# Sorting the listed columns of a sparse graph kernel by the half of the block's rows they reach, and multiplying half-width tiles in layer 2

## The chip, the cores and the metric

The kernel runs on one core of a Trainium2 chip. The metric is the time on the device in microseconds. The kernel before took 1107.85 us (median of three runs, 1107.15 to 1109.62). The profile is one further execution under the profiler, which took 1219.48 us; its span is 1217.8 us. A timed run is thus some 110 us shorter than what the profile shows.

## The reference, cut to what matters

The input is a feature matrix x of 2708 rows and 512 columns, and a sparse adjacency matrix adj (2708 x 2708) whose row density falls from the first rows to the last. Four layers follow each other, each of them x = layernorm(x + layer(x, adj)):

```python
# layer 0: normalized adjacency, then a projection
h = (d[:, None] * (adj + eye) * d[None, :]) @ x @ W.T + b
# layer 1: adj plus a head weight where adj > 0, by the degree
(inc @ x) / inc.sum(axis=1)
# layer 2: two gated branches over the same adj
h = x @ W_sa
e = where(adj != 0, exp(-leaky_relu(s_left[:, None] + s_right[None, :], 0.01)), 0)
x_a = (e / (e.sum(axis=1) + 1e-5)) @ h
x_b = adj @ (x @ W_gcnb) + b_gcnb
sigmoid(attn_a * x_a + attn_b * x_b)        # attn_* are gates from adj @ x and x
# layer 3: signs of x times signs of the weight, then adj, then relu
relu(adj @ (max(sign(x), 0) @ sign(weight).T))
```

All of it is fp32. Layer 2 needs, for each row, two weighted sums over its neighbours: one with the weights adj and one with the weights e.

## The kernel before, in words

Rows are cut into 22 blocks of 128 (the last has 20). For each block b other than 0 the kernel finds the columns of adj in which any of the block's 128 rows has an entry, lists them, and from then on works only on these. The list is padded to a fixed number of tiles of 128 columns, ROOM[b], from 9 for block 1 down to 4 and 1; in all there are 107 listed tiles. A few blocks treat block 0's columns (and block 1 its own) as whole tiles as well, which DIRECT names; block 0 itself uses all columns. A block's own diagonal is handled apart where it is the only entry (own_by_itself).

**First stage.** A loop of turns, one block per turn (function turn), reads adj in row blocks and finds the lists. Its instructions keep their written order on each engine (in_order). For a block, mark writes a 0/1 mask of the row block, and 22 products with a column of ones (line 801) count for each column how many of the block's rows have an entry. For a group of up to three blocks (GROUPS), count turns these counts into hits, numbers them with a scan along the free axis (line 820), and builds a table; count_partitions (line 833) adds the partitions in front; steps_of takes differences between partitions (line 849); look_up compares slot numbers with each partition's start (line 865) and multiplies (line 870) so that each slot of the list learns which column it holds. list_nodes writes the indices, and POOL then gathers the listed columns of adj (line 928) into packed[b]. The same turns transpose and project x for layer 0 (lines 943 and 958).

**Layers 0 and 1** gather feature rows by the indices (line 570) and multiply each tile of packed[b] with them.

**Layer 2** (function parts_of_sums and what follows) cuts a block's tiles into parts of up to three tiles. prepare makes, for one part, a buffer ae with two halves for each tile: adj itself and the weights e. The work is done by weights_of (lines 1326 to 1330: score plus bias on ScalarE, leaky relu, mask and sum on VectorE, exp on ScalarE), a copy (line 1474) and a reduction into esum (lines 1476 to 1487). There are three ae buffers. accumulate multiplies: add_products (line 1337) takes a gathered tile of 128 feature rows as the stationary operand, in four column chunks, and moves both halves of ae past it, 2 x 128 columns, into the accumulator acc. Gathered rows come by POOL's indirect DMA (line 1492) into seven buffers. project2 then copies acc to SBUF (pt, line 1520), multiplies with wab (pc, line 1527), W_gcnb and W_sa (pg and ph, line 1534), finish2 gates and normalizes (with a power on POOL, line 621), and sign_product (lines 1578 and 1583) prepares layer 3. Two parts of the next block are prepared ahead of the present block's projections in program order; the engines then run in the order that a scheduler gave their instructions at compile time.

**Layer 3** multiplies by tiles of the same packed[b] (lines 1694 and 1736).

Of the kernel before, what the change touches and what calls it, by code (L numbers as in the profile page):

```python
# [8 lines left out]
F32 = mybir.dt.float32  # L9
# [25 lines left out]
          13: (0,), 14: (0,), 15: (0,), 16: (0,), 17: (0,)}  # L35

# [449 lines left out]
def sparse_layers(ctx, tc, x, adj, adj_t, w0_t, b0, w_sa, a_sa, w_gcnb, b_gcnb, wa, ba, wb, bb, w3_t,  # L486
# [9 lines left out]

    nc = tc.nc
# [44 lines left out]
    ones_b = const.tile([P, 1], BF16, name="s_ones_b")  # L542
    nc.vector.memset(ones_b, 1.0)
# [6 lines left out]
    found = const.tile([P, NB], F32, name="s_found")  # L550
# [95 lines left out]
    l01 = ctx.enter_context(ExitStack())  # L646
    heads = l01.enter_context(tc.tile_pool(name="s_heads", bufs=1, reuse_waits="tile"))
    head_row = heads.tile([P, N], F32, name="s_head_row")

    with tc.tile_pool(name="s_pre", bufs=1) as pre:  # L650
        TM = max(ROOM)
        TS = max(sum(ROOM[b] for b in g) for g in GROUPS)
        GM = max(len(g) for g in GROUPS)
        NT = NB + 3
# [47 lines left out]
        )  # L702
        step = pre.tile([P, P], BF16, name="s_step")
# [3 lines left out]
        )  # L707
        off_dia = pre.tile([P, P], BF16, name="s_off_dia")
# [12 lines left out]
        lane_i = pre.tile([P, GM], I32, name="s_lane_i")  # L721
        nc.gpsimd.iota(lane_i, pattern=[[0, GM]], base=0, channel_multiplier=1)
        lane = pre.tile([P, GM], BF16, name="s_lane")
        nc.vector.tensor_copy(lane, lane_i)
        keep = pre.tile([P, GM, NB], BF16, name="s_keep")
# [38 lines left out]

        search = {}
        group_of = {b: g for g in GROUPS for b in g}

        def mark(b: int):
# [4 lines left out]
            if i == 0:  # L773
                find = ps_s.tile([P, D], F32, tag="find", name=f"find{b}", bufs=2)
                n = len(g)
                search[g] = {
                    "hits": find[:, : n * NB].rearrange("p (g s) -> p g s", g=n),
                    "before": find[:, n * NB : n * (NB + 1)],
                    "diff": find[:, D // 2 : D // 2 + n * NT],
                }  # L780
# [19 lines left out]
            for s in range(NB):  # L800
                nc.tensor.matmul(
                    search[g]["hits"][:, i, s : s + 1], mask[:m, s * P : (s + 1) * P], ones_b[:m],
                    start=True, stop=True,
                )

        def own_diagonal(b: int):

            if own_by_itself(b):
                g, m = group_of[b], rows(b)
                nc.vector.scalar_tensor_tensor(  # L810
                    dia_own[:m, b : b + 1], search[g]["hits"][:m, g.index(b), b : b + 1], 0.0,
                    dia[:m, b : b + 1], op0=ALU.is_equal, op1=ALU.mult,
                )

        def count(g):
            b0_, G = g[0], len(g)
            hit = small.tile([P, GM, NB], BF16, tag="hit", name=f"hit{b0_}")
            nc.vector.tensor_scalar(hit[:, :G], search[g]["hits"], 0.0, None, op0=ALU.is_gt)
            turn = small.tile([P, GM, NB], F32, tag="turn", name=f"turn{b0_}")
            nc.vector.tensor_tensor_scan(  # L820
                turn[:, :G].rearrange("p g s -> p (g s)"),
                keep[:, :G].rearrange("p g s -> p (g s)"),
                hit[:, :G].rearrange("p g s -> p (g s)"), 0.0, op0=ALU.mult, op1=ALU.add,
            )
            nc.vector.tensor_copy(found[:, b0_ : b0_ + G], turn[:, :G, NB - 1])
            table = small.tile([P, GM, NT], BF16, tag="table", name=f"table{b0_}")
            nc.vector.tensor_tensor(table[:, :G, :NB], turn[:, :G], hit[:, :G], op=ALU.mult)
            nc.vector.tensor_copy(table[:, :G, NB + 2], lane[:, :G])
            search[g].update(table=table)

        def count_partitions(g):
            b0_, G = g[0], len(g)
            nc.tensor.matmul(
                search[g]["before"], tri, found[:, b0_ : b0_ + G], start=True, stop=True
            )

        def steps_of(g):
            b0_, G = g[0], len(g)
            table, diff = search[g]["table"], search[g]["diff"]
            base = small.tile([P, 2, GM], F32, tag="base", name=f"base{b0_}")  # L840
            nc.vector.tensor_copy(base[:, 0, :G], search[g]["before"])
            nc.vector.tensor_scalar(
                base[:, 1, :G], base[:, 0, :G], WHOLE128, WHOLE128, op0=ALU.add, op1=ALU.subtract
            )
            nc.vector.tensor_copy(table[:, :G, NB], base[:, 1, :G])
            nc.vector.tensor_tensor(
                table[:, :G, NB + 1], base[:, 0, :G], base[:, 1, :G], op=ALU.subtract
            )
            nc.tensor.matmul(
                diff, step, table[:, :G].rearrange("p g c -> p (g c)"), start=True, stop=True  # L850
            )
            search[g]["base"] = base

        def look_up(g):
            b0_, G = g[0], len(g)
            base, diff = search[g]["base"], search[g]["diff"]
            steps = small.tile([P, GM, NT], BF16, tag="steps", name=f"steps{b0_}")
            nc.scalar.copy(steps[:, :G], diff.rearrange("p (g c) -> p g c", g=G))
            looked = ps_s.tile([P, D], F32, tag="looked", name=f"looked{b0_}", bufs=1)
            T = sum(ROOM[b] for b in g)  # L860
            lv = looked[:, : T * NT].rearrange("p (t c) -> p t c", t=T)
            after = pre.tile([P, TS * P], BF16, tag="after", name=f"after{b0_}", bufs=1)
            at = 0
            for i, b in enumerate(g):
                nc.vector.tensor_scalar(
                    after[:, at * P : (at + ROOM[b]) * P], slot[:, : ROOM[b] * P],
                    base[:, 0, i : i + 1], None, op0=ALU.is_ge,
                )
                for t in range(at, at + ROOM[b]):
                    nc.tensor.matmul(  # L870
                        lv[:, t, :], after[:, t * P : (t + 1) * P], steps[:, i, :],
                        start=True, stop=True,
                    )
                at += ROOM[b]
            search[g]["looked"] = lv
# [257 lines left out]
        room = pre.tile([1, NB], F32, name="s_room")  # L1133
        for b in range(NB):
            nc.vector.memset(room[:, b : b + 1], float(P * ROOM[b]))
        tot = ps_s.tile([P, D], F32, tag="find", name="tot", bufs=2)
        nc.tensor.matmul(tot[0:1, :NB], ones, found, start=True, stop=True)
        n_over = const.tile([1, 1], F32, name="s_n_over")
        nc.vector.tensor_tensor(room, tot[0:1, :NB], room, op=ALU.is_gt)
        nc.vector.tensor_reduce(n_over, room, axis=AX.X, op=ALU.add)  # L1140

    work = ctx.enter_context(tc.tile_pool(name="s_work", bufs=2, side="right", reuse_waits="tile"))
# [189 lines left out]
    def add_products(b: int, src, ae, r: int, is_first: bool, is_last: bool):  # L1332

        m = rows(b)
        acc = state[b]["acc"]
        for k in range(KC):
            nc.tensor.matmul(  # L1337
                acc[:, k, :].rearrange("p (h i) -> p h i", h=2)[:, :, :m],
                src[:r, k * P : (k + 1) * P], ae[:r, :, :m],
                start=(is_first and k % 2 == 0), stop=(is_last and k % 2 == 1),  # L1340
            )
# [17 lines left out]
    with tc.tile_pool(name="s_l1", bufs=8, reuse_waits="tile") as lp:  # L1359
# [4 lines left out]
        def grow2(j: int, n: int):  # L1364
# [15 lines left out]
            add_products(0, f[j], ae, r, n == 0, n == NB - 1)  # L1380
# [36 lines left out]
    with tc.tile_pool(name="s_l2o", bufs=1, reuse_waits="tile") as op, \  # L1417
# [6 lines left out]

        def parts_of_sums(b: int):

            runs = [(i, min(CH, tiles(b) - i)) for i in range(0, tiles(b), CH)]
# [4 lines left out]
        def prepare(b: int, c: int):  # L1432
# [5 lines left out]
            if run is None:  # L1438
# [3 lines left out]
                st["own_ae"] = ae  # L1442
# [14 lines left out]
                nc.scalar.activation(ae[:m, 1, :m], ident[:m, :m], AF.Copy, scale=own[:m, 4:5])  # L1457
                st["ae"][c] = ae
                return
            i0, n = run  # L1460
            nd = len(direct(b))
            for i in range(i0, i0 + n):
# [4 lines left out]
            a = packed[b][:, i0 : i0 + n, :]  # L1467
            ae = lp.tile([P, CH, 2, P], F32, tag="ae", name=f"ae{b}_{i0}", bufs=3)
            av, ev = ae[:, :n, 0, :m], ae[:, :n, 1, :m]
            weights_of(  # L1470
                ev, av, sl[:, :m], a, [st["src"][i][:, D : D + 1] for i in range(i0, i0 + n)],
# [3 lines left out]
            if i0 == 0:  # L1475
# [3 lines left out]
                if own_by_itself(b):  # L1479
                    own_e = st["own_ae"][:m, 1, :m]  # L1480
                    nc.vector.tensor_tensor(esum[:m, :m], esum[:m, :m], own_e, op=ALU.add)
            else:
                part = lp.tile([P, P], F32, tag="part", name=f"part{b}_{i0}")
                nc.vector.tensor_reduce(
                    part[:, :m, None], ev.rearrange("p t i -> p i t"), axis=AX.X, op=ALU.add
                )
                nc.vector.tensor_tensor(esum[:, :m], esum[:, :m], part[:, :m], op=ALU.add)
# [10 lines left out]
        def accumulate(b: int, c: int):  # L1498
# [6 lines left out]
            if run is None:  # L1505
                add_products(b, f[b], ae, m, True, last)
                return
            i0, n = run
            for i in range(n):
                add_products(  # L1510
                    b, st["src"][i0 + i], ae[:, i], P, c == 0 and i == 0, last and i == n - 1
# [312 lines left out]
```

## Time and profile before

| | value |
|---|---|
| timed, median of three | 1107.85 us |
| span of the profiled run | 1217.8 us |
| TensorE busy | 1007.9 us, 83% |
| VectorE busy | 726.2 us, 60% |
| POOL busy | 533.5 us, 44% |
| ScalarE busy | 403.4 us, 33% |
| products of line 1337 on gathered tiles | 856 instructions, 187.9 us |
| chain that ended last | PE 31%, DVE 5%, DMA 5% |

The profile's lines name an engine (PE is TensorE, PEld its weight loads, DVE VectorE, ACT ScalarE, POOL GpSimd), a line of the kernel, what is written from what, the shapes, the count, the busy time with the mean duration of one, and the idle time ahead with what ended it. Busy time of products is counted from their issue to their modelled end, and successive products overlap, so a product's mean duration is not the pace at which they follow each other. The chain is followed back from the last instruction to what released it at each step. The page also cuts the span into 40 slices with one digit of busy share each.

### The profile page before, as it was taken

To read this page: it belongs to the slowest core of one execution; us is meant where nothing else is said; L and a number is where in the kernel's file an instruction comes from. 1 tells how busy PE (TensorE), PEld (TensorE's weight loads), DVE (VectorE), ACT (ScalarE), POOL (GpSimd) and SP (SyncE) were. 2 spreads that over 40 slices of the span, in tenths; PEclk is the share of its full clock that TensorE was granted. 3 is DMA by queue.
4 is the path that set the end of the run, shared out by engine and by line. 5 is a ranking of instruction groups with operands and counts; after the bars stand their busy time and mean duration, and the time that the engine had idled before them with its cause. 6 is when DMAs were issued, how large, how long until landed. Compare 5 with 4: busy or idle time off the path is not lost. (4 is left out here: it accounts for less than half of the span.)

```text
span 1217.8 us, 13502 instructions
## 1 busy us (share of the span) xinstructions
PE 1007.9 (83%) x4009; PEld 608.2 (50%) x4028; DVE 726.2 (60%) x2556; ACT 403.4 (33%) x869; POOL 533.5 (44%) x545
## 2 busy tenths in 40 slices
PE   3865677579789789989799999999999999698852
PEld 2432333123334234445566677676666666476631
DVE  4764556464567676778656655656555554346765
ACT  4542444100000044668533223223232322243420
POOL 0455544676666377675332233222221211066660
PEclk9877778789799899999899999999999999889976
DMA  9875775476677677776332223223121211199982
GB/s 330 297 230 182 222 228 157 113 243 200 199 201 224 188 202 207 216 218 205 87 84 75 66 74 97 65 57 88 51 85 40 79 40 53 57 338 287 256 238 80
DMA packets 84523, 193.53 MB, mean 159 GB/s; under 512 B 13680, under 2 KB 26968, under 8 KB 84440
## 3 DMA queue, kind: packets, MB, share of 16 engines
q0 software_dynamic: 41056, 113.12, 33.8%
q1 hardware_dynamic: 31692, 64.45, 15.5%
q10 hardware_dynamic: 11692, 15.01, 3.8%
q8 instruction: 34, 0.56, 0.2%
q14 instruction: 49, 0.40, 0.1%
HBM read 155.73 MB, written 25.92 MB: 149 GB/s over the span
## 5 line engine op out<-in xcount | busy, mean ns | idle before, releaser
L1492 POOL DMA_INDIRECT xg<-x_rows,i x107 | 106.1, 991 | 216.9 <-DVE mv L619 63.3
L1337 PE MATMUL acc<-ae,xg 128*128 128x256 f32 x856 | 187.9, 378 | 0.4 <-ACT ae L1330 0.3
L1337 PEld LDWEIGHTS acc<-ae,xg 128*128 128x128 f32 x856 | 161.9, 190 | 23.0 <-ACT ae L1330 1.1
L928 POOL DMA_INDIRECT a<-in_adj_t_dram,row_at x107 | 110.2, 1030 | 128.6 <-DVE mask L782 83.6
L570 POOL DMA_INDIRECT xg<-x_rows,i x107 | 113.0, 1056 | 57.3 <-issue 26.2
L570 POOL DMA_INDIRECT xg<-y_rows,i x107 | 105.6, 987 | 53.3 <-issue 24.3
L1398 PE MATMUL l<-xg,inc 128*128 128x512 f32 x214 | 103.0, 617 | 15.6 <-DMA xg<-x_rows,i 12.4
L1254 PE MATMUL l<-xg,a 128*128 128x512 f32 x214 | 109.6, 645 | 7.6 <-issue 4.1
L570 POOL DMA_INDIRECT xg<-xw_rows,i x83 | 82.9, 998 | 46.1 <-issue 20.4
L958 PE MATMUL y<-s_w,xt 128*128 128x512 f32 (+1 forms) x176 | 96.1, 692 | 2.2 <-issue 2.0
L1534 PE MATMUL pg<-s_wg,pt 128*128 128x512 f32 (+1 forms) x176 | 82.7, 611 | 0.0
L1534 PE MATMUL ph<-s_wsa,pt 128*128 128x512 f32 (+1 forms) x176 | 79.3, 592 | 0.0
L621 POOL TENSOR_TENSOR rs<-mv,s_neg_half 128x1 f32<-128x1 f32 (+1 forms) x22 | 13.1, 596 | 150.8 <-DVE mv L619 150.5
L1398 PEld LDWEIGHTS l<-xg,inc 128*128 128x128 f32 x214 | 39.6, 194 | 72.2 <-issue 41.9
L1326 ACT ACTIVATE ae<-sl,xg 128x128 f32<-128x128 f32 x107 | 40.5, 394 | 99.8 <-DMA xg<-x_rows,i 88.6
L1337 PE MATMUL acc<-ae,f 128*128 128x256 f32 (+1 forms) x272 | 67.2, 390 | 7.4 <-ACT ae L1375 5.9
L1327 DVE SCALAR_TENSOR_TENSOR ae<-ae 128x128 f32<-128x128 f32 (+4 forms) x69 | 29.1, 422 | 66.8 <-ACT ae L1326 62.0
L1254 PEld LDWEIGHTS l<-xg,a 128*128 128x128 f32 x214 | 40.3, 202 | 56.7 <-issue 45.8
L1337 PEld LDWEIGHTS acc<-ae,f 128*128 128x128 f32 (+1 forms) x272 | 52.1, 195 | 25.3 <-issue 7.8
L958 PEld LDWEIGHTS y<-s_w,xt 128*128 128x128 f32 (+1 forms) x176 | 37.7, 227 | 50.7 <-issue 50.5
L615 DVE BATCH_NORM_STATS2 st<-t 128x6 f32<-128x512 f32 (+1 forms) x88 | 60.6, 689 | 1.2
L733 ACT ACTIVATE unused<-arow 128x1408 uint8<-128x1408 f32 (+3 forms) x44 | 58.3, 1326 | 0.9
(250 smaller groups left out, 1749.0 us busy)
## 6 DMA issues: line engine op xcount, KB each, us to landing
arow<-in_adj_dram SPq DMA_DIRECT2D x21, 704.0 KB
arow<-in_adj_dram SPq DMA_DIRECT2D x21, 650.0 KB
x_rows<-f SPq DMA_DIRECT2D x21, 258.0 KB
aw<-in_adj_t_dram SPq DMA_DIRECT2D x21, 256.0 KB
out_dram<-o SPq DMA_DIRECT2D x21, 256.0 KB
f<-in_x_dram SPq DMA_DIRECT2D x20, 256.0 KB
y_rows<-yt ACTq DMA_DIRECT2D x20, 256.0 KB
x_rows<-f SPq DMA_DIRECT2D x20, 256.0 KB
```

Source lines behind the costliest of these rows:

```text
L570: nc.gpsimd.indirect_dma_start(out=t[:, :dst_w], out_offset=None, in_=src[:, :], in_offset=bass.IndirectOffsetOnAxis(ap=index[b][:, i : i ...
L615: nc.vector.bn_stats(st[:m], t[:m])
L733: nc.scalar.activation(unused[:m, : ar.shape[1]], ar, AF.Copy, accum_out=row_sums[:m, b, h : h + 1])
L928: nc.gpsimd.indirect_dma_start(out=packed[b][:, t + len(direct(b)), :], out_offset=None, in_=adj_t, in_offset=bass.IndirectOffsetOnAxis(ap ...
L958: nc.tensor.matmul(ps[:m], xt[:, k, :m], w0[:, k, :], start=(k == 0), stop=(k == KC - 1))
L1254: nc.tensor.matmul(ps[:m], packed[b][:, i, :], moving[:, :D], start=(i == 0), stop=(i == len(src) - 1),)
L1326: nc.scalar.activation(ev[:, i, :], sl, AF.Identity, bias=score)
L1327: nc.vector.scalar_tensor_tensor(ev, ev, SLOPE, ev, op0=ALU.mult, op1=ALU.max)
L1337: nc.tensor.matmul(acc[:, k, :].rearrange("p (h i) -> p h i", h=2)[:, :, :m], src[:r, k * P : (k + 1) * P], ae[:r, :, :m], start=(is_first ...
L1398: nc.tensor.matmul(ps[:m], inc[:, i, :m], src[i0 + i][:, :D], start=(i0 + i == 0), stop=(i0 + i == len(src) - 1),)
L1492: nc.gpsimd.indirect_dma_start(out=g, out_offset=None, in_=x2_rows[:, :], in_offset=bass.IndirectOffsetOnAxis(ap=index[b][:, t : t + 1], a ...
L1534: nc.tensor.matmul(ps[:m], pt[:, k, h, :m], w[:, k, :], start=(k == 0), stop=(k == KC - 1))
```

## The change

A listed column need not have entries in both halves of the block's 128 rows. The change sorts each block's list by kind: first the columns with entries in rows 0 to 63 only (upper), then those with entries in both halves, then those with entries in rows 64 to 127 only (lower). For each block HALVES gives how many tiles at the front are sure to hold only upper columns and how many at the back only lower ones. In layer 2 such a tile has nothing in the other half of the rows, so its ae needs only 2 x 64 columns, and its products move 128 columns in place of 256 into the matching half of acc. Parts become runs of tiles of one kind.

To find the kinds, the counting products of the first stage use three columns (upper, lower, all) in place of one; count builds three kinds of hits with a scan each; the bases, tables and differences are three (four) times as wide; look_up adds up to three terms for each slot, with a comparison for each kind. Checks at the end of the stage compare the number of columns of each kind with what HALVES promises. The flag that leads to the dense fallback is set from them, as before. The list's length, the gathers and the other layers' tiles are the same in number.

The diff, cut to its core:

```diff
+HALVES = ((0, 0), (3, 4), (3, 3), (2, 3), (2, 2), (2, 3), (2, 2), (2, 2), (2, 2), (2, 2), (2, 2),
+          (2, 2), (2, 2), (1, 1), (1, 1), (1, 2), (1, 2), (1, 2), (1, 1), (1, 2), (1, 2), (0, 0))
+HALF = 64
...
+    sides = const.tile([P, 3], BF16, name="s_sides")
...
+    found = const.tile([P, 3, NB], F32, name="s_found")
...
-                    search[g]["hits"][:, i, s : s + 1], mask[:m, s * P : (s + 1) * P], ones_b[:m],
+                    search[g]["hits"][:, i, s, :], mask[:m, s * P : (s + 1) * P], sides[:m],
...
+                own = search[g]["hits"][:m, g.index(b), b, :]
+                nc.vector.scalar_tensor_tensor(
+                    own[:, 0:2], sides[:m, 0:2], own[:, 2:3], own[:, 0:2],
+                    op0=ALU.mult, op1=ALU.add,
+                )
...
+            nc.vector.tensor_tensor(both, side[0], side[1], op=ALU.mult)
+            nc.vector.tensor_tensor(upper, side[0], both, op=ALU.subtract)
+            nc.vector.tensor_tensor(lower, side[1], both, op=ALU.subtract)
+            for c in range(3):
+                nc.vector.tensor_tensor_scan(
+                    turn[:, c, : G * NB], keep[:, :G].rearrange("p g s -> p (g s)"),
+                    kind[:, c, : G * NB], 0.0, op0=ALU.mult, op1=ALU.add,
+                )
...
+            nc.tensor.matmul(before, tri, counts, start=True, stop=False)
+            nc.tensor.matmul(before[:, 1:], all_ones, counts[:, :2], start=False, stop=False)
+            nc.tensor.matmul(before[:, 2:], all_ones, counts[:, :1], start=False, stop=True)
...
+                for c, (t0, t1) in enumerate(((0, T - nl), (nu, T - nl), (nu, T))):
+                    nc.vector.tensor_scalar(
+                        after[:, at_a * P : (at_a + t1 - t0) * P], slot[:, t0 * P : t1 * P],
+                        base[:, 0, c * G + i : c * G + i + 1], None, op0=ALU.is_ge,
+                    )
...
-                acc[:, k, :].rearrange("p (h i) -> p h i", h=2)[:, :, :m],
-                src[:r, k * P : (k + 1) * P], ae[:r, :, :m],
+                acc[:, k, :].rearrange("p (h i) -> p h i", h=2)[:, :, at[0] : at[1]],
+                src[:r, k * P : (k + 1) * P], ae[:r],
...
+        def span(b: int, i: int):
+            t, (nu, nl) = i - len(direct(b)), HALVES[b]
+            if 0 <= t < nu:
+                return 0, HALF
+            return (HALF if t >= ROOM[b] - nl else 0), rows(b)
...
-            runs = [(i, min(CH, tiles(b) - i)) for i in range(0, tiles(b), CH)]
+            runs = []
+            for i in range(tiles(b)):
+                if runs and runs[-1][2] == span(b, i) and runs[-1][1] < CH:
+                    i0, n, at = runs.pop()
+                    runs.append((i0, n + 1, at))
+                else:
+                    runs.append((i, 1, span(b, i)))
...
-                nc.scalar.activation(ae[:m, 1, :m], ident[:m, :m], AF.Copy, scale=own[:m, 4:5])
+                nc.scalar.activation(esum[:m, :m], ident[:m, :m], AF.Copy, scale=own[:m, 4:5])
+                nc.scalar.copy(ae[:m, 1, :m], esum[:m, :m])
...
-            a = packed[b][:, i0 : i0 + n, :]
-            ae = lp.tile([P, CH, 2, P], F32, tag="ae", name=f"ae{b}_{i0}", bufs=3)
+            a = packed[b][:, i0 : i0 + n, r0:r1]
+            ae = lp.tile([P, CH * 2 * P], F32, tag="ae", name=f"ae{b}_{i0}", bufs=3)
...
+            elif n == 1:
+                nc.vector.tensor_tensor(
+                    esum[:, r0:r1], esum[:, r0:r1], ev[:, 0, :], op=ALU.add
+                )
```

The memory of head_row is taken after the first stage's pool is given back, in place of before it, and the number of buffers of a few small tiles is set to two.

## The prediction

> **What bounds the kernel now.** I read the page's busy shares and slices first, then sums by stage, then the chain of waits inside layer 2, then single instructions.
>
> ```profile
> PE 1007.9 (83%) x4009; PEld 608.2 (50%) x4028; DVE 726.2 (60%) x2556; ACT 403.4 (33%) x869; POOL 533.5 (44%) x545
> PE   3865677579789789989799999999999999698852
> DVE  4764556464567676778656655656555554346765
> PEclk9877778789799899999899999999999999889976
> ```
>
> TensorE is at nine tenths over slices 20 to 34 (layer 2) and lower elsewhere. The sums by stage (stretch, its length, then busy time of PE, PEld, DVE, ACT, POOL, then clock, DMA share, GB/s):
>
> ```profile
> 0.00:240.00 240.00, 156.60 (x908) 78.69 (x908) 135.03 (x590) 96.78 (x175) 112.12 (x119) 0.83 0.68 218
> ...
> 575.00:1062.00 487.00, 460.47 (x1898) 320.10 (x1915) 276.51 (x829) 152.03 (x378) 119.17 (x129) 0.99 0.25 69
> ```
>
> The change touches two stages. In layer 2 (575 to 1062) TensorE is busy 95% at full clock, VectorE 57%, DMA 25%. In the first stage (0 to 240: read adj, list columns) nothing is full on average, but its undisturbed turns look different:
>
> ```profile
> 55.37:60.89 5.52, 3.72 (x29) 2.52 (x30) 5.35 (x25) 4.10 (x7) 4.43 (x4) 0.73 0.87 246
> 85.98:91.50 5.52, 3.85 (x30) 2.51 (x30) 5.31 (x23) 4.10 (x7) 4.43 (x4) 0.74 0.88 253
> ```
>
> In these turns (one block each, from mask to mask) VectorE is busy 97%. Other turns last 12 to 17 us, with waits that the profile gives to "remote" (48.6 us at ScalarE's copy xt alone). One period of layer 2, in the chain in order of time:
>
> ```profile
> 917.97 5.08 PE acc L1337 x24
> 923.05 3.65 DMA xg<-x_rows,i
> ...
> 929.07 0.61 PE pc L1527 x4
> 930.27 0.81 PE px L1583 x3
> 931.42 3.54 PE pg L1534 x8
> 934.96 3.43 PE ph L1534 x8
> 938.50 5.08 PE acc L1337 x24
> ```
>
> A period of 20.5 us: 9.1 us of acc, then 9.5 us of fixed TensorE work (tb, px, pc, pg, ph, half of the own tile). The remaining 1.9 us is a wait: a gather for the next block starts only behind the POW of the layernorm on POOL, lands after 3.65 us, and ScalarE serves the next block's ae before it copies pt, for which pc waits. So layer 2 is bound by TensorE with about 2 us of latency per block on top.
>
> ```profile
> 900.06 7.07 PE L1337 MATMUL acc<-ae,xg 128*128 128x256 f32 x32
> ...
> 908.54 0.61 PE L1527 MATMUL pc<-s_wab,pt 128*128 128x2 f32 x4 [0.48 <-ACT pt L1520]
> ```
>
> The mean of 378 ns in the group is a latency; the pace is (7.07 - 0.38) / 31 = 216 ns for each of the 8 instructions of a tile (4 products, two instructions each), so 1.73 us a tile.
>
> [...] The trace has 128-column fp32 products with a fresh load each: the transposes of line 943 start 109 ns apart. [...] the pc products of line 1527, with 2 moving columns, start 112 ns apart, so a load costs 112 and no more is hidden. [...]
>
> **The change part by part.**
>
> Removed, layer 2: HALVES sums to 34 upper and 42 lower tiles, so 76 of 107 listed tiles move 128 columns instead of 256. That is 608 instructions. The price lies between 109 ns (the product) and 125 ns (my allowance if load and product overlap imperfectly); I take 112, the load. 608 x (216 - 112) = 63 us, from 55 to 65.
>
> Does it reach the end? The compiled order of instructions shows what stands ahead of the pt copy on ScalarE. Before, in a five-tile block, it is the next block's ae from a gather issued behind the POW: pt starts 10.6 us after ph ends (4.2 to the POW, 0.6 POW, 0.5, 3.65 landing, 0.4 + 0.9 + 0.4 for ae, rest hand-over). After, the part ahead of pt is smaller. For blocks 13 to 17 it comes from a gather issued a block earlier; the limit is VectorE's own queue, about 7.5 us: t 0.75, t 0.69, statistics 1.0, f 0.56, bx 0.43, with two small ae parts of about 1.0 to 1.3 each and waits. TensorE's own acc there is 9.1 - 3 x 0.83 = 6.6 us. So the period falls by about 2.9 us, not only by 2.5. For blocks 3, 5, 6, 9 the part ahead of pt still comes from a gather behind the POW (pt at 9 to 11.5 us), saving 2.2 to 3.2; blocks 2, 4, 7, 8 save 4.4 to 4.8; 10 to 12 about 3.0; 18 to 20 about 1.9; block 1, with its 9 gathered tiles for 7 buffers, 4. The sum over blocks is 62 us. Each of these counts a queue on VectorE as if nothing slipped; I take off 7 and use 55, with 28 as the low end if VectorE's queue costs another 1.4 us in each of 19 blocks.
>
> Added, layer 2: more and smaller parts. Block 15 goes from two (384 and 256 columns) to four (128, 64, 128, 128). On VectorE: before, 5 operations near 0.55 + 5 near 0.37 + one 0.29, 5.0 us; [...] Equal, and inside the periods already counted. The own tile writes esum on ScalarE and copies it, one more 0.28 us copy; ScalarE is busy 31% of the stage. With three ae buffers and four parts, the fourth part waits until TensorE has finished the first: 2.2 us after ph ends. Behind that wait on VectorE stand the layernorm's aggregate and mv. It ends about 0.2 us after the preceding statistics, so I price it at 0 to 0.3 us in ten blocks, within the 7 above.
>
> Added, first stage, all on VectorE:
>
> ```profile
> L865 DVE TENSOR_SCALAR after<-s_slot,base 128x512 bf16<-128x512 int16 x8 | 2.6, 374 | 0.0
> L820 DVE TENSOR_TENSOR_SCAN turn<-s_keep,hit 128x66 f32<-128x66 bf16 x5 | 1.5, 296 | 0.1
> L827 DVE TENSOR_TENSOR table<-turn,hit 128x66 bf16<-128x66 f32 x5 | 1.2, 233 | 0.0
> ```
>
> count: two more scans (0.59), [...] a table three times as wide (+0.14), hit twice as wide (+0.06): 1.3 us for a group of three, 1.15 and 0.95 for two and one, 10.7 in all. look_up: two more L865 per block, 0.2 us of start cost each (the rows run 254 ns at 128 columns, 515 at 1152, and overlap some 0.05), 42 of them: 8.4; and 62 more tiles, 3T - 2 x halved instead of T, at 0.033: 2.1. own_diagonal: 20 more at 0.16: 3.2. Together 24.4 us. On TensorE 62 more look-up products at 26 ns and some fp32 counts, under 6 us, behind the projections of line 958 in its queue; ScalarE's steps is four times as wide, +0.2 in nine groups, beside VectorE. The limits at the end exchange 22 memsets for some 23 and ten tiny operations: about 1 us.
>
> How much shows? Where a turn is undisturbed, VectorE sets it and the cost comes through whole (24). Where adj's loads or the "remote" waits set it, it hides. At 0.88 DMA share the loads are close behind: 5.5 us turns could hardly go under 4.9. I take 15, with 5 and 30 as ends [...].
>
> Moved: head_row's place, found's layout, the order of listed columns. Layers 0, 1 and 3 process as many tiles as before, with the same widths: nothing.
>
> Sum: 1107.85 - 55 + 15 = 1068.
>
> **The rivals.** (1) VectorE's queue and the smaller lead of two parts prepared ahead become layer 2's bound: gain 28, cost 15, 1095. For: VectorE holds every part's ae and the layernorm in one queue. Against: 57% busy. (2) The first stage hides its additions and layer 2 gives all: gain 62, cost 5, 1051. For: its mean VectorE share is 56%. Against: the 97% turns. (3) The first stage pays 30 and small parts leave only 25: 1113, slower. For: the 5.5 us turns, and a profiled run 110 us longer than the timed one, so the timed one may have fewer hiding waits. Against: TensorE's queue in layer 2 is full and 63 us leave it.
>
> **How the numbers follow.** Forecast 0.60, rival 1 0.17, rival 2 0.16, rival 3 0.07. The range goes from rival 2's 1051 less a little, 1048, to rival 1's 1095. Faster by over 0.2% (2.2 us): 0.91, the first three less a little; within 0.2%: 0.02; slower: 0.07.
>
> **What would show it.** 128x128-form products at line 1412 starting 109 to 115 ns apart; periods of about 17.5 us in blocks 13 to 17; pc's wait for pt not longer than now; VectorE about 24 us busier before 240 us and the stage some 15 longer. Wrong would be: halved products starting 150 ns or more apart, TensorE idle before acc for ae, or first-stage turns longer by over 1.3 us each.

## The result, and the profile after

The changed kernel takes 1056.55 us (median of four runs, 1055.49 to 1059.00), the kernel before 1107.88 in the same comparison: a ratio of 0.9538, 95% interval 0.9516 to 0.9560, or 51 us less (49 to 54). The forecast was 1068, with 1048 to 1095 as its range.

The profiled run of the kernel before was 110 us longer than its timed runs, so I set the changed kernel beside a second profile of before, whose span is 1106.0 us and is called "before" from here on. The page of the changed kernel, in the same views as those shown ahead (busy shares, then slices):

```profile
PE 922.5 (87%) x4125; PEld 556.7 (53%) x4144; DVE 721.2 (68%) x2799; ACT 409.5 (39%) x915; POOL 540.7 (51%) x546
...
PE   2988897489998798999799998999999999799972
...
DVE  4899999365787586898566555665566654368965
...
PEclk9998999799999799999999999999999999989986
```

TensorE is still the fullest engine: from slice 21 to slice 34 (counted from 1) it stands at eight or nine tenths. VectorE is now at nine tenths in slices 3 to 7, the first stage. The two stages by sums (stretch, length, busy PE, PEld, DVE, ACT, POOL, clock, DMA share, GB/s), first before, then after; the second row runs from the end of ph of block 21 to that of block 20, so it holds 19 periods of layer 2:

```profile
0.00:200.00 200.00, 147.30 (x933) 75.06 (x934) 146.76 (x652) 97.73 (x178) 127.74 (x129) 0.90 0.85 283
557.40:963.10 405.70, 392.60 (x1633) 276.57 (x1650) 228.66 (x673) 119.20 (x300) 99.75 (x109) 1.00 0.25 67
```

```profile
0.00:200.00 200.00, 148.03 (x1031) 78.61 (x1031) 166.84 (x757) 98.66 (x177) 127.81 (x125) 0.92 0.85 277
562.30:915.50 353.20, 338.50 (x1637) 237.67 (x1654) 205.46 (x786) 122.17 (x342) 100.54 (x109) 0.99 0.28 77
```

Layer 2 gives 405.7 - 353.2 = 52.5 us in these 19 blocks. With blocks 0, 1 and 21 (from the first acc product on) it is 597.5 against 542.6, or 54.9. VectorE does 20 us more in the first 200 us (18 in the first 240), but layer 0's first gather starts only 6.1 us later (187.4 and 193.5). The first acc product starts 7.3 us later. Layer 3 is nearly the same (131.7 and 130.1 us from its first product on).

Two periods of layer 2 after, in the chain in order of time (start, length, what):

```profile
795.84 7.40 PE acc L1412 x42
803.64 0.97 PE acc L1412 x4
804.95 0.54 PE acc L1412 x2
805.54 0.81 PE px L1678 x3
806.69 3.54 PE pg L1629 x8
810.23 3.43 PE ph L1629 x8
813.77 4.80 PE acc L1412 x26
818.59 0.59 POOL rs L632
819.21 0.60 DVE f L642
821.58 0.56 ACT pt L1615
822.19 0.61 PE pc L1622 x4
```

The first period (block 14, 17.9 us) is TensorE alone; the gather link (3.65 us of landing) that stood in the same place before is gone. In the second (block 15, also 17.9 us) the chain leaves TensorE through the POW of the layernorm (rs, line 632), f on VectorE and pt on ScalarE. TensorE waits for that pt:

```profile
815.77 4.57 PE L1412 MATMUL acc<-ae,xg 128*128 128x128 f32 x32
...
822.19 0.61 PE L1622 MATMUL pc<-s_wab,pt 128*128 128x2 f32 x4 [0.68 <-ACT pt L1615]
```

The 32 products of this block's listed tiles are 24 halved and 8 whole ones (the timeline names only the first form). In the trace the 531 halved products of these periods that are followed by another acc product start 112.3 ns apart on average (median 112), the whole ones at a median of 216: 24 x 112 + 8 x 216 = 4.42 us, and the last product, a halved one, lasts 275 ns where its spacing is 112, which brings it to the 4.57 shown.

### The profile page after: what moved, and what is told of

Read it like the earlier page. It is cut to its first block, busy times and chain, and to the rows that moved or that the text cites. A ratio compares the mean times of both kernels' runs of the same rounds, so it can differ in the third digit from the quotient of the medians.

```text
span 1057.2 us, 14099 instructions
## 1 busy us (share of the span) xinstructions
PE 922.5 (87%) x4125; PEld 556.7 (53%) x4144; DVE 721.2 (68%) x2799; ACT 409.5 (39%) x915; POOL 540.7 (51%) x546
## 3 DMA queue, kind: packets, MB, share of 16 engines
q1 hardware_dynamic: 31692, 64.45, 17.8%
## 5 line engine op out<-in xcount | busy, mean ns | idle before, releaser
L983 POOL DMA_INDIRECT a<-in_adj_t_dram,row_at x107 | 119.9, 1120 | 70.0 <-DVE deg L760 37.7
L1412 PE MATMUL acc<-ae,xg 128*128 128x128 f32 (+1 forms) x856 | 125.4, 305 | 5.9 <-ACT ae L1406 5.9
L1412 PEld LDWEIGHTS acc<-ae,xg 128*128 128x128 f32 x856 | 117.2, 191 | 15.1 <-ACT ae L1406 8.2
L1330 PE MATMUL l<-xg,a 128*128 128x512 f32 x214 | 104.3, 615 | 21.5 <-DMA xg<-y_rows,i 21.0
L581 POOL DMA_INDIRECT xg<-xw_rows,i x83 | 82.3, 992 | 32.6 <-issue 13.1
L1013 PE MATMUL y<-s_w,xt 128*128 128x512 f32 (+1 forms) x176 | 87.6, 645 | 0.0
L1473 PEld LDWEIGHTS l<-xg,inc 128*128 128x128 f32 x214 | 40.1, 195 | 66.0 <-issue 36.1
L1330 PEld LDWEIGHTS l<-xg,a 128*128 128x128 f32 x214 | 37.7, 191 | 70.1 <-issue 44.1
L1402 ACT ACTIVATE ae<-sl,xg 128x64 f32<-128x64 f32 (+1 forms) x107 | 35.9, 362 | 53.5 <-DMA xg<-x_rows,i 28.2
L1831 PE MATMUL l<-xg,p 128*128 128x512 f32 (+1 forms) x166 | 48.4, 423 | 9.1 <-DMA xg<-xw_rows,i 8.0
L1629 PEld LDWEIGHTS ph<-s_wsa,pt 128*128 128x128 f32 (+1 forms) x176 | 32.7, 186 | 42.8 <-issue 42.6
```

Source lines behind the costliest of these rows:

```text
L581: nc.gpsimd.indirect_dma_start(out=t[:, :dst_w], out_offset=None, in_=src[:, :], in_offset=bass.IndirectOffsetOnAxis(ap=index[b][:, i : i ...
L983: nc.gpsimd.indirect_dma_start(out=packed[b][:, t + len(direct(b)), :], out_offset=None, in_=adj_t, in_offset=bass.IndirectOffsetOnAxis(ap ...
L1013: nc.tensor.matmul(ps[:m], xt[:, k, :m], w0[:, k, :], start=(k == 0), stop=(k == KC - 1))
L1330: nc.tensor.matmul(ps[:m], packed[b][:, i, :], moving[:, :D], start=(i == 0), stop=(i == len(src) - 1),)
L1412: nc.tensor.matmul(acc[:, k, :].rearrange("p (h i) -> p h i", h=2)[:, :, at[0] : at[1]], src[:r, k * P : (k + 1) * P], ae[:r], start=(is_f ...
L1473: nc.tensor.matmul(ps[:m], inc[:, i, :m], src[i0 + i][:, :D], start=(i0 + i == 0), stop=(i0 + i == len(src) - 1),)
```

## Where the time went: which part of the change does what

Four runs separate the parts. The first is the kernel before, unchanged.

> The kernel before, unchanged, for a second profile: its profiled run was 110 us longer than its timed runs. Expected 1107 to 1110 us and, if the profile is not lengthened this time, stage times that can be set beside those of the changed kernel: turns of the first stage near 5.5 to 6.5 us throughout if the additions cost there (changed kernel: 7.3 mean), or near 7 if the loads of adj set the pace anyway and the additions hide.

It took 1107.84 us. VectorE's turns in the first stage are 7.2 us on average (143.6 us from the first of 21 masks to the last, 20 turns), against 7.7 after (153.3 us; the 7.3 above divided by one turn too many): 0.5 more, although the new work is some 20 us, or 1.0 a turn.

Next, the changed kernel with layer 2 at full width:

```diff
-            if 0 <= t < nu:
-                return 0, HALF
-            return (HALF if t >= ROOM[b] - nl else 0), rows(b)
+            return 0, rows(b)
```

> Sorted lists as in the changed kernel, but layer 2 takes every tile at full width in parts of up to three, so only the cost of sorting is left. My forecast (the first stage pays 15): 1123 us. Rival, the first stage hides the additions: 1108 to 1113. Rival, it pays 30: 1138. Given the changed kernel's 1056.6, a value near 1112 would mean that the halved tiles alone give 55.

It took 1123.47 us, ratio 1.0163 (1.0135 to 1.0191): 16 us slower than before. That looks like my 15, but the profile puts only 6.3 us of it ahead of the first acc product. 7.5 us lie in layer 2, 4.4 of them in the 19 periods, where pc's wait for pt grew by 2.4 (below); for the rest no cause is shown. A difference of whole times was thus no measure of the first stage.

Then parts cut by kind, but every product at full width:

```diff
-                if runs and runs[-1][2] == span(b, i) and runs[-1][1] < CH:
+                if runs and span(b, runs[-1][0]) == span(b, i) and runs[-1][1] < CH:
...
-                    runs.append((i0, n + 1, at))
+                    runs.append((i0, n + 1, (0, rows(b))))
...
-                    runs.append((i, 1, span(b, i)))
+                    runs.append((i, 1, (0, rows(b))))
```

> Sorted lists, parts cut by kind as in the changed kernel, but all at full width: more and smaller parts without narrower products. If smaller parts cost layer 2 (VectorE's queue, the lead of two parts, rival 1), this is 10 to 27 us above the kernel with sorted lists and parts of three; by my forecast the cost is within 0 to 7 us.

It took 1107.02 us (0.9990, 0.9971 to 1.0008): 16 us faster than with parts of three. Smaller parts don't cost; they gain what the sorting costs. What TensorE waited for in the 19 periods (waiting line, what for, sum in us, times, longest) shows where, first before, then sorted lists at full width in parts of three, then parts cut by kind:

```profile
PE pc L1527 <- ACT pt L1520: 11.9, 18, 1.1
```

```profile
PE pc L1620 <- ACT pt L1613: 14.3, 18, 2.1
```

```profile
PE pc L1622 <- ACT pt L1615: 1.5, 4, 0.7
```

The wait for pt is almost gone without a single narrower product. In the changed kernel, part of the waiting is back:

```profile
PE pc L1622 <- ACT pt L1615: 5.5, 8, 1.1
PE px L1678 <- ACT xt L1675: 3.3, 2, 1.7
PE acc L1412 <- ACT ae L1406: 2.9, 3, 1.9
PE tb L1673 <- DVE bx L1665: 1.8, 4, 0.8
```

So the sum over 19 periods runs: 405.7 before, 410.1 with sorted lists in parts of three, 393.3 with parts by kind, 353.2 with narrow products. The last step removes 552 x 104 ns = 57.4 us from TensorE and yields 40.1; 17 us are given back, 12 of them as TensorE's idle time (2.8 to 14.7), since with less to multiply TensorE comes earlier to nearly the same queues (42 gathered tiles stand ahead of pt at full width, 41 in the changed kernel; how they are counted comes below).

Up to 3.4 of the 17 us are TensorE's granted clock. In these profiles it is either full or half (1.0 or 0.5). In the 19 periods it is full throughout before and with parts by kind at full width; in the changed kernel it is half twice, for 3.41 us each time, in blocks 6 and 11. Block 11 then takes 19.6 us; in a run with the same layer 2 and no such stretch there (the changed kernel with 63 more comparisons, below) it takes 17.8. Each stretch thus costs some 1.7 us. Why it comes, no run here shows.

Last, layer 2 of the changed kernel behind the first stage of the kernel before (line by line the two sources; no further edit):

> First stage of the kernel before, layer 2 of the changed kernel. Without sorted lists the halved tiles leave out entries of the other half, so this computes less than the reference; it shows layer 2's gain without the sorting's cost. Forecast (layer 2 gives 55, sorting costs 15): 1053 if layer 2 gives just that, with the changed kernel then 15 above; since the changed kernel is at 1056.6, this should be at 1042 to 1046 if sorting costs 10 to 15, and at 1052 to 1056 if the first stage hides it.

It took 1049.41 us, ratio 0.9477 (0.9452 to 0.9503). Sorting therefore costs 7 us in the changed kernel, though with these intervals it could be 3 to 10. The profiles agree: with the first stage as it was, layer 0's first gather starts at 184.9 to 187.8 us (three profiles, the next run's among them), with sorting and nothing else in that stage at 192.9 to 195.5 (seven); the first acc product starts 6.9 us later on average. My 15 was about twice too much.

**Is it smaller parts by themselves?** The kernel before with CH = 2 in place of 3:

> The kernel before with parts of at most two tiles in place of three: no sorting, no narrow products. If smaller parts by themselves shorten pc's wait for pt (11.9 us in 18 blocks before, 1.5 with parts cut by kind at full width), this gives 8 to 14 us: 1094 to 1100. If the gain of the parts cut by kind came from another thing in the sorted kernel: 1106 to 1110. If smaller parts overload VectorE's queue: above 1112.

1095.60 us, 0.9893 (0.9862 to 0.9924): 12 us from one constant, without sorting. The 19 periods take 393.3 us, as many as with parts cut by kind at full width, and the wait falls nearly as much:

```profile
PE pc L1527 <- ACT pt L1520: 2.5, 7, 0.5
```

## Why the first stage hides two thirds of VectorE's additions

I had taken VectorE's 97% busy turns as the limit. In the undisturbed profile (the second one of before) VectorE is busy 107 of the 120 us from 40 to 160, and another engine has no time left. POOL fetches the listed tiles of adj one by one; in the first stage of before (busy us, mean ns, then idle ahead and what ended it):

```profile
L928 POOL DMA_INDIRECT a<-in_adj_t_dram,row_at x107 | 116.6, 1090 | 68.6 <-DVE mask L782 36.6 <-issue 29.6 <-DMA a<-in_adj_t_dram,row_at 1.8
```

```profile
L983 POOL DMA_INDIRECT a<-in_adj_t_dram,row_at x107 | 119.9, 1120 | 70.0 <-DVE deg L760 37.7 <-issue 29.9 <-DVE f L1034 0.6
```

The first wait, 36.6 us, is for the first list. From there (39.3 us in both) the 107 fetches follow each other until 189.6 in before: 116.6 busy + 29.6 between them = 146.2 of 150.3 us. POOL waits for other engines and transfers for less than 3 us in between, so VectorE's turns have slack as long as they bring lists faster than POOL fetches them. With sorting, the fetches start more than 2 us apart in six places in place of two, and the last ends 3.7 us later (3.3 of it are longer fetches, 119.9 in place of 116.6 us; why they are longer isn't shown). The other 2.5 of the 6.1 us are order: on POOL, the last fetch stands behind layer 0's first gather before, and ahead of it after.

TensorE is a rival, with 111 of those 120 us busy. But it has done its part early: ahead of layer 0's products it stands idle for gathered rows, in before 18.8 us in one piece (13.5 after):

```profile
L1254 PE MATMUL l<-xg,a 128*128 128x512 f32 x214 | 105.1, 627 | 25.2 <-DMA xg<-y_rows,i 25.2
```

Test: 63 more comparisons ahead of the real ones in the look-up, 20 us of VectorE, once in the kernel before and once in the changed one:

```diff
+                for _ in range(3):
+                    nc.vector.tensor_scalar(
+                        again, slot[:, : 3 * P], base[:, 0, i : i + 1], None, op0=ALU.is_ge
+                    )
```

> The kernel before with three more comparisons of 128x384 per block ahead of the real one in the look-up: 63 instructions of 316 ns, 20 us more on VectorE in the first stage, as much as the sorting adds there. If POOL's chain of 107 fetches of adj tiles (1.4 us each, back to back from 39 us on in the undisturbed profile of before) sets the end of the stage, most is hidden: 1111 to 1115 us. If VectorE's turns set it, as I assumed for undisturbed turns: 1123 to 1128. If adj's loads set it: 1108 to 1110.

1118.11 us, 1.0081 (1.0049 to 1.0114): +10 us, between my two values.

> The changed kernel with the same 63 comparisons, 20 us, added once more. VectorE is busy 37 of 40 us in its turns and POOL's fetches already wait in five places, so the slack should be used up: 1070 to 1077 us if POOL's chain was what hid the first 20. If the loads of adj hide them, or half of them always hides: 1057 to 1066.

1072.13 us, 0.9670 (0.9641 to 0.9699): 15.6 us above the changed kernel. POOL's chain in the two:

```profile
L933 POOL DMA_INDIRECT a<-in_adj_t_dram,row_at x107 | 114.7, 1072 | 74.4 <-DVE mask L783 38.7 <-issue 29.0 <-DVE base L842 4.6
```

```profile
L988 POOL DMA_INDIRECT a<-in_adj_t_dram,row_at x107 | 116.6, 1090 | 88.5 <-DVE deg L761 40.2 <-issue 29.0 <-DVE find L837 8.9
```

The first 20 us of extra VectorE work move layer 0's start by 3.8 us, the second 20 by 14.1 (193.5 to 207.6), with POOL now waiting for lists; the last fetch moves by 3.9 and by 16.7. That is what a slack used up looks like, and it speaks against adj's loads as the limit: the share of the DMA engines in the first 240 us falls from 0.84 in the changed kernel to 0.79 in the last one while the stage grows. Also, in before the rows of the last block that is listed are loaded and masked by 147.3 us, 42 us ahead of the last fetch's end. Of the +10 us in before, only 3.8 are in the first stage; the rest is spread over later layers, whose code is the same. I can't say from what; its profiled run was 4 us above its median, and in the 19 periods it has one stretch at half clock, which the run without the extra work has not.

## What bounds layer 2 now

In the second period shown above, pt stands on ScalarE behind the exp of the next block's second ready part (start, length, instruction, idle time ahead):

```profile
821.41 0.26 ACT L1406 ACTIVATE ae<-ae 128x64 f32<-128x64 f32 x1 [2.47 <-DVE ae L1405]
821.57 0.57 ACT L1615 COPY pt<-acc 128x512 f32<-128x512 f32 x1
```

and that exp waits for VectorE, whose queue holds the layernorm first:

```profile
819.21 0.60 DVE L642 TENSOR_SCALAR f<-t,mv,rs 128x512 f32<-128x512 f32 x1 [1.26 <-POOL rs L632]
...
819.93 0.41 DVE L1665 TENSOR_SCALAR bx<-f 128x512 bf16<-128x512 f32 x1
...
821.09 0.23 DVE L1405 TENSOR_TENSOR ae<-ae 128x64 f32<-128x64 f32 x1
```

pt starts 7.8 us after ph ends (813.76), where I had 7.5. The order of ScalarE's instructions, fixed at compile time, tells how many gathered tiles of the next block must be scored ahead of pt, for blocks 2 to 19:

```
before          5 5 5 5 5 5 5 5 5 5 4 4 4 4 4 4 4 4   sum 82
before, CH = 2  3 4 3 4 4 3 3 4 4 4 3 3 3 3 3 4 4 4   sum 63
changed         2 4 2 4 4 2 2 3 3 3 1 1 1 1 1 3 2 2   sum 41
```

A tile ahead of pt has to be gathered, land, be scored and pass VectorE before TensorE may go on. Next come runs that move this number. Three parts prepared ahead, parts of at most two tiles, four ae buffers:

```diff
-        CH = 3
+        CH = 2
...
-            ae = lp.tile([P, CH * 2 * P], F32, tag="ae", name=f"ae{b}_{i0}", bufs=3)
+            ae = lp.tile([P, CH * 2 * P], F32, tag="ae", name=f"ae{b}_{i0}", bufs=4)
...
-        AHEAD2 = 2
+        AHEAD2 = 3
```

> The changed kernel with three parts prepared ahead in place of two, parts of at most two tiles and four ae buffers (of two tiles' size, as memory allows). Rival 1 said that the smaller lead of two parts would bound layer 2: then this is 4 to 10 us faster, 1046 to 1052. My view: a third part ahead puts its gather, which waits behind the POW, ahead of pt on ScalarE again, and pc's wait for pt grows from 5.5 to 12 us or more: 1060 to 1070.

1062.31 us, 0.9586 (0.9554 to 0.9617), 6 us slower than the changed kernel. The order now has 61 tiles ahead of pt, and the wait is back:

```profile
PE pc L1622 <- ACT pt L1615: 11.4, 13, 1.8
PE px L1678 <- ACT xt L1675: 4.3, 3, 1.6
```

Then one edit at a time, all on another chip, where before took 1109.72. Only CH = 2:

> The changed kernel with parts of at most two tiles. Only blocks 1 to 9 have runs of three alike tiles, so this touches few parts. If smaller parts shorten the wait for pt here as they did without sorting (12 us over all blocks), up to 4 us: 1052 to 1056. If VectorE's queue is near its limit in the early blocks, up to 4 us slower: 1057 to 1061.

1056.29 us (five runs, 1055.01 to 1058.89): no difference to the changed kernel, and its order has the same 41 tiles. CH = 2 and four ae buffers, two parts ahead:

> As the changed kernel with parts of at most two tiles, and four ae buffers in place of three, still two parts prepared ahead. If the fourth part's wait for a free ae buffer holds up the layernorm behind it on VectorE (I priced it at 0 to 0.3 us in ten blocks), 1 to 3 us faster than with three; if it costs nothing, the same within 1 us; together with the run with three parts ahead this tells whether that one lost by its lead or by its buffers.

1064.81 us (five runs, 1064.36 to 1069.71), 8.5 us slower than with three (1.7 of it, in the profiles, one more stretch at half clock). I had expected a small gain or nothing. The order is that of the run with three parts ahead, 61 tiles, and so is the wait:

```profile
PE pc L1622 <- ACT pt L1615: 11.3, 13, 1.6
PE px L1678 <- ACT xt L1675: 4.7, 3, 1.7
```

With four buffers it thus makes no difference whether two or three parts are named as ready (three named with three buffers was not run); the step from three buffers to four changes what stands ahead of pt. The fourth part's wait for a buffer, which I had priced as a cost, keeps that part behind pt and so helps. CH = 2 with eight buffers for gathered rows in place of seven, three ae buffers:

> As the changed kernel with parts of at most two tiles, and eight buffers for gathered rows in place of seven. If what is left of TensorE's idle time in layer 2 (about 15 us in 19 blocks) comes from gathers that start late because a buffer is not yet free, 3 to 8 us faster than with seven: 1046 to 1053. If the gathers wait for the POW ahead of them on POOL, no difference: 1054 to 1059.

1051.38 us (five runs, 1049.23 to 1054.54), ratio to before 0.9479 (0.9451 to 0.9507). Its range lies wholly below that with seven. The 19 periods take 346.0 us, against 353.2, first with seven buffers, then with eight:

```profile
562.10:915.30 353.20, 339.88 (x1635) 238.59 (x1653) 207.50 (x806) 122.83 (x348) 100.47 (x109) 0.99 0.28 77
559.10:905.10 346.00, 335.58 (x1635) 236.00 (x1653) 207.20 (x806) 122.80 (x348) 99.69 (x108) 1.00 0.28 78
```

What TensorE waits for with eight:

```profile
PE pc L1622 <- ACT pt L1615: 5.5, 9, 1.5
PE tb L1673 <- DVE bx L1665: 1.8, 4, 0.8
```

The waits for pt and bx are as with seven buffers (5.5 and 1.8 us); the wait of px for xt, 3.4 us with seven, is gone. That is half of the 7 us. But TensorE, which does the same products, is also busy 4.3 us less: the profile with seven buffers has three stretches at half clock (0.99 on average), the one with eight none (1.00), and three, at the 1.7 us estimated above, cost some 5 us. The two causes overlap, and how much of the gain the eighth buffer makes by itself is thus open. This is the fastest version found.

Last, the same with parts of one tile (CH = 1), 27 tiles ahead of pt:

> As the run with eight buffers for gathered rows, but parts of one tile, three ae buffers of one tile each. In the compiled order of ScalarE the tiles of the next block that stand ahead of pt fall from 41 to 27 over 18 blocks (82 in the kernel before). If their number sets pc's wait for pt and nothing else does, that wait falls from 5.5 to below 2 us: 1045 to 1050. Rival 1's lead: with two to three single tiles prepared (some 0.9 us of TensorE for a halved one), TensorE waits for ae inside acc instead, and the many small operations fill VectorE: 1056 to 1075.

It ran on a chip on which the kernel before, too, took 1210.93 us, so its 1173.53 us (0.9674, 0.9629 to 0.9719) can't be set beside the others; its layer 2 can, with that caution. The 19 periods take 356.3 us, 10 more than in the run above:

```profile
PE acc L1412 <- ACT ae L1406: 9.6, 9, 1.7
PE acc L1412 <- ACT ae L1402: 1.8, 2, 1.2
...
PE pc L1622 <- ACT pt L1615: 0.9, 2, 0.8
```

Both theories were half right: fewer tiles ahead of pt do end its wait (0.9 us), and with parts of single tiles TensorE waits inside acc instead (11.4 us), as rival 1 had it. The changed kernel sits between the two.

## Why the prediction was right, point by point

- **The price of a halved product.** Right: 112.3 ns against 112. pc's products, in which only 2 columns move, also start 112 ns apart (median), while line 943's transposes, with 128 columns and a load each as here, start 109 apart at full clock. Whether the load or the product sets the pace of a halved product is thus not shown. 552 of the 608 instructions lie in the 19 periods and give 57.4 us.
- **The 1.9 us of waiting per block.** Too large by the trace: in the second profile of before TensorE is idle 13.1 us in 19 periods, 0.7 a block, 11.9 of it for pt.
- **Layer 2 gives 55.** Right, 54.9, but that it fits so closely is luck, for the steps inside differ. The sum over blocks of 62, less 7 for slips, came out as 52.5 for blocks 2 to 20, where the 62 held 58, and 2.4 for the rest, where block 1 alone had 4. By blocks: 2, 4, 7 and 8 save 3.8 to 4.7 (4.4 to 4.8 said); 3, 5, 6 and 9 save 1.8, 3.5, 1.2 and 3.0 (2.2 to 3.2); 10 to 12 save 3.0, 0.9 and 3.3 (3.0); without the half clock, which no term foresaw, 6 and 11 would save some 1.7 more; 13 to 17 fall to 18.1, not 17.5, from 20.4, saving 2.3, not 2.9. That smaller parts put a gather issued a block earlier ahead of pt was right, and is worth 12 us alone.
- **pc's wait for pt.** Not longer, as said: 5.5 us in place of 11.9. But TensorE idle before acc for ae, named as a sign of being wrong, did come, with 2.9 us.
- **VectorE in layer 2.** "Equal" was wrong: 228.7 to 205.5 us over 19 blocks, 1.2 us less a block. The added parts cost nothing in sum (229.3 at full width), the narrower ones save the 24. A 64-column operation of line 1405 takes 221 ns where a 128-column one takes 288; the price of 64 columns in the forecast was an assumption, for the profile ahead of it has no such operation.
- **The fourth part's buffer wait.** Wrong in sign: without it the kernel is 8.5 us slower.
- **The first stage: the mis-sized term.** VectorE's some 20 us more (18 by 240 us, where 24.4 were said) cost about 7 us, not 15. The price of three bf16 operations a group in the 24.4 was an assumption; for a group of three blocks they take 228, 228 and 221 ns (lines 850 to 852, 66 columns). I had let turns at 97% of VectorE pay in full and held adj's loads for the other limit; two turns of 5.5 us were no sample of a stage whose undisturbed mean is 7.2. POOL's 107 fetches at 1.4 us each, which in the lengthened profile were broken by waits of up to 11.4 us, set the end. This term is 8 of the 11 us between forecast and result. With it the sum is 1107.85 - 54.9 + 7.3 = 1060; of the other 3 to 4 us one or two are layer 3's, and the rest is within what single profiles and medians differ by (the two profiles lie 48.8 us apart, the medians 51.3).
- **The rivals.** Rival 2 came closest in time (1051): its 5 us for the first stage were nearer than my 15, but layer 2 did not give its 62. Rival 1's limit exists, but at the lead that the change leaves it costs little (the 2.9 us before acc). Rival 3 needed a first stage that pays 30.

## What to carry to other kernels

Before costing work added to a busy engine, look for a serial chain beside it (here 107 fetches on POOL, back to back) that ends later; additions hide behind it until its slack is used (3.8 of the first 20 us showed here at layer 0's start); after that most of each shows (14 of 20 us). When a product gets cheaper, ask what it had covered: of 57 us taken from TensorE 17 came back, most of it as waits, and only the smaller parts, which shortened the chain ahead of the copy that TensorE waits for, made up for it. More buffers can be slower (8.5 us here, with four in place of three), where a wait for a buffer had kept low-priority work behind urgent work in an engine's queue.

## What the runs showed of the hardware that was not expected

On one chip the kernel before took 1210.93 us, on three others 1107.6 to 1109.7. Part of the extra time is in the first stage, under waits that the profile calls "remote"; in the run with parts of one tile on that chip:

```profile
ACT xt L1005 <- remote: 47.4, 6, 22.6
```

There layer 0's first gather starts at 243.8 us, in the changed kernel at 193.5. The profile shown ahead of the prediction has the same waits (48.6 us at xt). Set beside the second profile of the same kernel, its 112 us more are 52 ahead of layer 0's first gather, 28 from there to the first acc product, 12 in layer 2 and 21 after it. What the waits are, the profile doesn't tell.
